# A graph layer's kernel: the experts' first rows prepared three chunks before the end of the node products

## The chip, the cores and the metric

The kernel runs on one core of one Trainium2 chip. The metric is the device time of one execution in microseconds. Three timed runs of the kernel before took 3494.83, 3513.76 and 3521.78 us; their median is 3513.76. One further execution was recorded by the hardware profiler, and its trace is what the text reads.

## What is computed

One layer of a graph network over 10000 rows of 512 numbers and 160000 weighted edges, in float32. Three parts follow each other: a graph product over the edges (a gather, a weighted sum by destination node, a product with W), a linear attention, and a mixture of experts whose weights are chosen once for the whole input.

```python
xn = _layernorm(x, axis=-1)
x = x + _L0_gnn_ref(xn, L0_gnn_W, L0_gnn_bias, edge_weight, src, dst) \
      + _L0_mix_ref((xn)[None], L0_mix_w_qkv, L0_mix_w_out, L0_mix_gamma)[0]
x = x + _L0_ffn_ref((_layernorm(x, axis=-1))[None], L0_ffn_router_w, L0_ffn_W1, L0_ffn_b1, L0_ffn_W2, L0_ffn_b2)[0]
```

Inside the graph product:

```python
h = jnp.matmul(X, W)
msgs = h[edge_src] * edge_weight[:, None]
agg = jax.ops.segment_sum(msgs, edge_dst, num_segments=X.shape[0])
return jax.nn.relu(agg + bias)
```

Inside the experts (six experts with a hidden width of 341 each; the kernel computes the first 1408 hidden units, eleven blocks of 128, for every row, and the rest only if the chosen weights need them):

```python
h = jax.nn.gelu(jnp.einsum('bsd,edf->ebsf', x, W1) + b1[:, None, None, :], approximate=False)
out_e = jnp.einsum('ebsf,efd->ebsd', h, W2) + b2[:, None, None, :]
return jnp.einsum('be,ebsd->bsd', expert_weights, out_e)
```

## The kernel before

**Tiles and stages.** Rows are worked on in 20 chunks, numbered 0 to 19: nineteen of 512 rows (128 partitions by 4 rows) and a last one of 272 (68 partitions). `NCH` is 20, so `NCH - 3` is chunk 17. The stages are: keys and queries with the first sums over edges; then, chunk by chunk, the attention's output (`attention`, products `po`), the node rows gathered from the edge sums (`gathered`, tile `at`), their transposition (`transposed`, `pt` to `aT`) and the node products with W (`pg`), which give the new rows `ot`, stored to DRAM as `x1_d` (`x_d` in the profile); then the experts, again chunk by chunk.

**The edges beside the chunks.** Until chunk 17 GpSimd gathers messages of 128 edges at a time (`msg`, line 584), TensorE sums them by a selection matrix (`pm`, line 602), ScalarE copies and stores the sums (`part`, lines 605 and 606). In the loop over chunks, chunk 17 begins with `all_edges_in` (defined above line 1014): the remaining edges are summed, the edge pools are closed, and `experts_weights` opens the pool of the experts' weights and loads them (sixteen loads of W1, line 305, one of W2, line 306, on SP). Then the last two chunks' node rows are gathered, and the attention of chunk 19 is computed with the transposition of chunk 17's rows in its middle.

**What a chunk ends with.** After its four node products a chunk adds bias, applies the ReLU and adds `ot` (lines 1090 and 1091), is stored (line 1092), and its mean and variance are found on VectorE with a square root on ScalarE (`row_stats`, lines 166 to 180, the root at 174). They are kept in `stats2`. A weighted sum of the rows goes to `xsum` (line 1103). Chunk 17 ends with `sums_of_weights`, four VectorE sums over W1 (lines 226 to 229 through the helper `sums_of`).

**The experts' rows.** The experts read the stored rows back in another layout: `rows_in` (line 328, four loads of 256 KB for a full chunk) brings them in squares of 32 by 32; `stats_of_squares` (line 337, four small TensorE products with the tile `squares`, and a ScalarE copy at 339) brings the statistics into the same layout; `normalising` (line 351) is sixteen ScalarE activations for a full chunk; `rows_turned` (line 367) is one VectorE transposition in blocks; `turned_in` (through `sums_for`, lines 233 to 236) makes four sums `xs`. The products of the experts use sums and differences of quarters, so they need both the rows `xnT` and the sums `xs`. `hidden` computes px, py and pz (all at line 243, the helper `product`), of which the last addition to px waits until VectorE has read it (`u`, lines 1290 and 1291). The activation function follows at line 1277.

**What sets the order.** TensorE runs in the order in which the program is written (`manual_schedule`). The other engines' orders come from a scheduler that ranks instructions by their place in the program and by when it expects them to be ready; each engine then runs its own queue in that order. Buffers are taken from pools in a stack; a tile that lies where a closed pool lay waits for the last users of that memory. Only the rows of chunk 0 are treated here: in the kernel before, their pool `f_in`, the tile `squares`, the loads, the normalising and the turning stand at the end of chunk 18 (lines 1110 to 1123):

```python
if c == NCH - 2:
    io_f["in"] = ctx.enter_context(tc.tile_pool(name="f_in", bufs=1, reuse_waits="tile"))
    ...
    xn = rows_in(0)
    ...
    turn = turned_in(0, rows_turned(0, xn))
```

The other chunks' rows are prepared inside the experts' loop, one chunk ahead.

Of the kernel before, what the change touches and what calls it, by code (L numbers as in the profile page):

```python
# [9 lines left out]
F32 = mybir.dt.float32  # L10
# [7 lines left out]
P = 128  # L18
SQ = 32
SPARE = 10  # L20
SUB = 4
# [35 lines left out]
def gps_layer_kernel(  # L57
# [19 lines left out]
    nc = tc.nc  # L77
# [19 lines left out]
    NCH = len(chunks)  # L97
# [6 lines left out]
    small = ctx.enter_context(tc.tile_pool(name="small", bufs=4))  # L104
# [3 lines left out]
    ident = const.tile([P, P], F32, name="ident")  # L108
# [181 lines left out]
    io_f = {}  # L290
    held_w = {}

    def experts_weights():
        wp = ctx.enter_context(tc.tile_pool(name="f_w", bufs=1, reuse_waits="tile"))
        w1_sb = held_w["w1"] = wp.tile([P, KB, NBASE * P], F32, name="w1_sb")
        w2_sb = held_w["w2"] = wp.tile([P, NBASE, D], F32, name="w2_sb")
        held_w["w1_sum"] = wp.tile([P, 4, KH, PAIRS * P], F32, name="w1_sum")
        b1_sb = held_w["b1"] = wp.tile([P, NF], F32, name="b1_sb")
        rw_sb = held_w["router"] = wp.tile([P, KB, NP], F32, name="rw_sb")
        nc.scalar.dma_start(rw_sb, router_t.rearrange("(k p) d -> p k d", p=P))  # L300
        nc.scalar.dma_start(b1_sb[:, : NF - 1], b1_a)
        nc.scalar.dma_start(b1_sb[: fsz[-1], NF - 1 :], b1_b)
        for j in range(KB):
            for g in range(P // SQ):
                nc.sync.dma_start(w1_sb[g * SQ : (g + 1) * SQ, j, :], features(w1)[j, g, :, : NBASE * P])
        nc.sync.dma_start(w2_sb, w2[: NBASE * P, :].rearrange("(f p) d -> p f d", p=P))
# [8 lines left out]
    def rows_in(c):  # L315

        r = chunks[c][1]
        xn = io_f["in"].tile([P, SUB, D], F32, name="xn2")
        if r % SQ:
            for j in range(KB):  # L320
                for g in range(P // SQ):
                    nc.sync.dma_start(xn[:r, :, j * P + g * SQ : j * P + (g + 1) * SQ],
                                      x1_d[c][:, :, g * P + j * SQ : g * P + (j + 1) * SQ])
        else:
            squares = x1_d[c].rearrange("(b t) s (g e) -> g t s b e", t=SQ, g=P // SQ)
            by = xn[:, :, : r // SQ * P].rearrange("p s (b e) -> p s b e", e=P)
            for g in range(P // SQ):
                nc.sync.dma_start(by[g * SQ : (g + 1) * SQ], squares[g])
        return xn

    def stats_of_squares(st, c0):


        n = st.shape[2]
        pst = psum.tile([P, P // SQ, n, SUB, 2], F32, name="pst", tag="ps")
        for b in range(P // SQ):
            nc.tensor.matmul(pst[:, b], io_f["squares"][:, b], stats2[:, c0 : c0 + n], start=True, stop=True,
                             skip_group_check=True)
        nc.scalar.copy(st, pst)

    def normalising(c, xn, st):

        r = chunks[c][1]

        def normal(s):
            if r % SQ:
                nc.scalar.activation(xn[:r, s, :], xn[:r, s, :], AF.Identity,
                                     bias=stats2[:r, c, s, 0:1], scale=stats2[:r, c, s, 1:2])
                return
            for b in range(r // SQ):  # L350
                nc.scalar.activation(xn[:, s, b * P : (b + 1) * P], xn[:, s, b * P : (b + 1) * P], AF.Identity,  # L351
                                     bias=st[:, b, s, 0:1], scale=st[:, b, s, 1:2])

        return [partial(normal, s) for s in range(SUB)]

    def rows_turned(c, xn):
        r = chunks[c][1]
        xnT = io_f["in"].tile([P, KB, SUB * P], F32, name="xnT")
        if r % SQ:
            for j in range(KB):  # L360
                pt = psum.tile([P, SUB * P], F32, name="pt", tag="ps")
                for s in range(SUB):
                    nc.tensor.transpose(pt[:, s * r : (s + 1) * r], xn[:r, s, j * P : (j + 1) * P],
                                        ident[:r, :r])
                (nc.scalar.copy if j % 2 else nc.vector.tensor_copy)(xnT[:, j, : SUB * r], pt[:, : SUB * r])
        else:
            nc.vector.transpose(
                xnT[:, :, : SUB * r].rearrange("p j (m t) -> p m j t", t=SQ),
                xn[:, :, : r // SQ * P].rearrange("p s (b j e) -> p (s b) j e", j=KB, e=SQ))
        return xnT  # L370

    def turned_in(c, xnT):
        h = 2 * chunks[c][1]
        xs = io_f["in"].tile([P, 4, KH, HALF], F32, name="xs")
        sums_for([xs[:, i, :, :h] for i in range(4)], xnT[:, :KH, :h], xnT[:, :KH, h : 2 * h],
                 xnT[:, KH:, :h], xnT[:, KH:, h : 2 * h])
        return xnT, xs
# [10 lines left out]
    with ExitStack() as ph:  # L388
# [222 lines left out]
        held = {"edges": []}  # L611
# [243 lines left out]
        xn = rows_of(0)  # L855
# [150 lines left out]
        def all_edges_in():  # L1006
            edges_to(NQ)
            carry(CARRIES[-1], NW - 1)
            assert not carried
            pools.clear()  # L1010
            edge_ctx.close()
            experts_weights()

        def gathered(c):
# [49 lines left out]
        for c, (_, r) in enumerate(chunks):  # L1064
            ot, at = mixed.pop(0), ats.pop(0)
            aT = io.tile([P, KB, SUB * P], F32, name="aT", bufs=1)

            if c == NCH - 3:
                all_edges_in()
                ats += [gathered(c + 1), gathered(c + 2)]  # L1070

            def nodes_rows():
                transposed(aT, at, r, psum, "ps", by_act=range(KB))

            if c + MIXED < NCH - 1:
                mixed.append(attention(c + MIXED, nodes_rows))
            elif c == NCH - 3:
                mixed.append(attention(NCH - 1, nodes_rows))
            else:
                nodes_rows()  # L1080
            if c < NCH - 3:
                ats.append(gathered(c + 1))
            if c == NCH - 4:
                held["last"] = queries_in(NCH - 1), rows_again(NCH - 1)

            for s in range(SUB):
                po = psum.tile([P, D], F32, name="pg", tag="ps")
                times(po, aT, s, r, wg)
                put_out(KB * PRODUCT)
                nc.vector.tensor_tensor(po[:r, :], po[:r, :], bias_b[:r], ALU.add)  # L1090
                nc.vector.scalar_tensor_tensor(ot[:r, s, :], po[:r, :], 0.0, ot[:r, s, :], op0=ALU.max, op1=ALU.add)
            nc.sync.dma_start(x1_d[c], ot[:r])
            mv = stats2[:, c]
            row_stats(ot, r, mv)

            if c == NCH - 1:
                normalize(wg, ot, r, mv)

            nc.vector.scalar_tensor_tensor(mv[:r, :, 0], mv[:r, :, 0], -1.0, mv[:r, :, 1],
                                           op0=ALU.mult, op1=ALU.mult)  # L1100
            if c < NCH - 1:
                for s in range(SUB):
                    nc.vector.scalar_tensor_tensor(xsum[:r], ot[:r, s, :], mv[:r, s, 1:2], xsum[:r],
                                                   op0=ALU.mult, op1=ALU.add)
                moved = small.tile([P, 1], F32, name="moved")
                nc.vector.tensor_reduce(moved[:r], mv[:r, :, 0], axis=AX.X, op=ALU.add)
                nc.vector.tensor_tensor(msum[:r], msum[:r], moved[:r], ALU.add)
            if c == NCH - 3:
                sums_of_weights()
            if c == NCH - 2:  # L1110
                io_f["in"] = ctx.enter_context(tc.tile_pool(name="f_in", bufs=1, reuse_waits="tile"))

                io_f["squares"] = io_f["in"].tile([P, P // SQ, P], F32, name="squares")
                for b in range(P // SQ):
                    nc.vector.tensor_copy(
                        io_f["squares"][:, b].rearrange("k (g t) -> k g t", t=SQ),
                        ident[:, None, b * SQ : (b + 1) * SQ].to_broadcast([P, P // SQ, SQ]))
                xn = rows_in(0)
                st = small.tile([P, P // SQ, 1, SUB, 2], F32, name="st_sq", bufs=1)
                stats_of_squares(st, 0)  # L1120
                for step in normalising(0, xn, st[:, :, 0]):
                    step()
                turn = turned_in(0, rows_turned(0, xn))
        in_order.close()
        query_ctx.close()

# [347 lines left out]
```

## Time and profile before

| What | us |
|---|---|
| timed runs: lowest, median, highest | 3494.83, 3513.76, 3521.78 |
| the profiled execution | 3295.9 |
| its span from first to last instruction | 3294.2 |
| TensorE busy in it | 3187.5 |
| VectorE busy | 1772.1 |
| ScalarE busy | 834.1 |
| GpSimd busy | 1317.8 |

The profiled execution is shorter than the timed ones; its mean granted TensorE clock is 0.985. All times of the trace are counted from the start of its span. A matmul of float32 appears in the trace as two records. In a row of the timeline the columns are the start, the length, the engine, the source line, the operation with output and inputs, the shapes, the number of instructions merged, and in brackets the idle time before it with what ended it. `x_d` stands for all of `x1_d`, `w_sb` for W1's, W2's and the edges' weights, `xn` for the experts' rows too. The stage of the edges ends at about 1845 us, that of the node products at about 1905 us; the experts take the rest.

### The profile page before, as it was taken

How to read it: one execution, taken by the hardware profiler on the slowest of the kernel's cores; microseconds unless marked ns; L12 is line 12 of the kernel's file. 1: busy time of each engine (PE TensorE's matmuls, PEld its weight loads, DVE VectorE, ACT ScalarE, POOL GpSimd, SP SyncE). 2: the span in 40 equal slices, each digit the busy share in tenths (PEclk: the TensorE clock that was granted, in tenths of full speed). 3: DMA queues.
4: the chain of work that ended last, by engine and by line, in shares of the span. 5: the costliest groups of instructions: out<-in, count | busy, mean ns of one | idle time of the engine just before them, and what ended most of it. 6: DMA issues, size and time to landing. Idle time of an engine off the chain costs nothing. (4 is left out here: it accounts for less than half of the span.)

```text
span 3294.2 us, 35223 instructions
## 1 busy us (share of the span) xinstructions
PE 3187.5 (97%) x12819; PEld 1898.0 (58%) x12819; DVE 1772.1 (54%) x3902; ACT 834.1 (25%) x1674; POOL 1317.8 (40%) x1421
## 2 busy tenths in 40 slices
PE   5899999999999999999999979999999999999998
PEld 3344444444443333333333358888888888888886
DVE  6655555555555366666665665455544554445532
ACT  5422222222222122222222132222222222222211
POOL 3377777777776777777777200000000000000000
PEclk8899999999999999999999989999999999999999
DMA  9678889888888999999999822121212212121111
GB/s 391 245 238 282 265 274 311 265 281 255 283 267 240 344 353 355 337 350 351 354 338 313 230 67 62 52 90 52 64 52 76 66 52 64 52 90 51 54 38 41
DMA packets 216728, 654.33 MB, mean 199 GB/s; under 512 B 34425, under 2 KB 74361, under 8 KB 188831
## 3 DMA queue, kind: packets, MB, share of 16 engines
q0 software_dynamic: 104096, 354.29, 32.9%
q1 hardware_dynamic: 69992, 175.33, 16.2%
q10 hardware_dynamic: 42452, 122.31, 9.6%
q8 instruction: 105, 1.72, 0.2%
q14 instruction: 83, 0.68, 0.1%
HBM read 491.21 MB, written 166.63 MB: 200 GB/s over the span
## 5 line engine op out<-in xcount | busy, mean ns | idle before, releaser
L584 POOL DMA_INDIRECT msg<-xn_d,src_sb x1250 | 1237.6, 990 | 422.9 <-issue 318.4
L602 PE MATMUL pm<-msg,sel 128*32 128x512 f32 x2504 | 357.7, 604 | 15.4 <-DMA msg<-xn_d,src_sb 14.4
L209 PE MATMUL pg<-wq,aT 128*128 128x512 f32 (+1 forms) x640 | 292.2, 604 | 0.0
L209 PE MATMUL po<-G,qT 128*128 128x512 f32 (+1 forms) x640 | 290.3, 600 | 1.4 <-DMA qT<-qT_d 1.4
L912 PE MATMUL pc<-xn,ek 128*128 128x512 f32 (+1 forms) x640 | 285.5, 596 | 0.0
L605 ACT COPY part<-pm 128x512 f32<-128x512 f32 x217 | 127.0, 585 | 618.3 <-PE pm L602 577.4
L602 PEld LDWEIGHTS pm<-msg,sel 128*32 128x32 f32 x2504 | 67.0, 109 | 273.0 <-issue 190.5
L209 PEld LDWEIGHTS pg<-wq,aT 128*128 128x128 f32 (+1 forms) x640 | 115.5, 188 | 176.1 <-issue 161.2
L243 PE MATMUL px<-xnT,w_sb 128*128 128x256 f32 (+1 forms) x800 | 204.9, 379 | 7.0 <-DVE u L1291 6.6
L209 PEld LDWEIGHTS po<-G,qT 128*128 128x128 f32 (+1 forms) x640 | 114.8, 187 | 164.7 <-issue 157.8
L166 DVE BATCH_NORM_STATS2 st<-ot 128x6 f32<-128x512 f32 (+1 forms) x160 | 110.4, 690 | 180.1 <-ACT ot L1053 179.3
L243 PE MATMUL p<-kq_sum,xs_b 128*128 128x512 f32 (+1 forms) x432 | 200.7, 600 | 0.0
L912 PEld LDWEIGHTS pc<-xn,ek 128*128 128x128 f32 (+1 forms) x640 | 118.0, 191 | 139.3 <-issue 131.4
L243 PE MATMUL px<-w_sb,hh 128*128 128x256 f32 (+1 forms) x800 | 185.8, 379 | 0.0
L243 PE MATMUL py<-xs,w_sum 128*128 128x256 f32 (+1 forms) x800 | 185.7, 375 | 0.0
L243 PE MATMUL py<-w_sum,hh 128*128 128x256 f32 (+1 forms) x800 | 179.2, 379 | 0.0
L243 PEld LDWEIGHTS px<-xnT,w_sb 128*128 128x128 f32 x800 | 150.8, 192 | 30.1 <-DVE u L1291 10.2
L243 PEld LDWEIGHTS px<-w_sb,hh 128*128 128x128 f32 (+1 forms) x800 | 150.2, 188 | 22.8
L243 PEld LDWEIGHTS py<-w_sum,hh 128*128 128x128 f32 (+1 forms) x800 | 150.0, 188 | 22.7
L243 PEld LDWEIGHTS py<-xs,w_sum 128*128 128x128 f32 x800 | 150.2, 191 | 20.1
L243 PEld LDWEIGHTS p<-kq_sum,xs_b 128*128 128x128 f32 (+1 forms) x432 | 78.0, 187 | 116.1 <-issue 89.6
L351 ACT ACTIVATE xn<-xn,st_all 128x128 f32<-128x128 f32 x288 | 114.8, 481 | 97.3 <-DMA xn<-x_d 97.3
(298 smaller groups left out, 4566.8 us busy)
## 6 DMA issues: line engine op xcount, KB each, us to landing
part_d<-part ACTq DMA_DIRECT2D x217, 256.0 KB
msg<-xn_d,src_sb POOLq DMA_INDIRECT x1250
xn<-in_x SPq DMA_DIRECT2D x19, 1024.0 KB
xn_d<-xn ACTq DMA_DIRECT2D x19, 1024.0 KB
qT_d<-qT ACTq DMA_DIRECT2D x19, 1024.0 KB
qT<-qT_d SPq DMA_DIRECT2D x19, 1024.0 KB
xt<-in_x SPq DMA_DIRECT2D x19, 1024.0 KB
x_d<-ot SPq DMA_DIRECT2D x19, 1024.0 KB
```

Source lines behind the costliest of these rows:

```text
L166: nc.vector.bn_stats(st[:r, s, :], t[:r, s, :])
L209: nc.tensor.matmul(po[:r, :], t[:, kb, s * r : (s + 1) * r], w[:, kb, :], start=kb == 0, stop=kb == KB - 1)
L243: nc.tensor.matmul(o, lhs[j], rhs[j], start=start and j == 0, stop=stop and j == n - 1, skip_group_check=True)
L351: nc.scalar.activation(xn[:, s, b * P : (b + 1) * P], xn[:, s, b * P : (b + 1) * P], AF.Identity, bias=st[:, b, s, 0:1], scale=st[:, b, s, ...
L584: nc.gpsimd.indirect_dma_start(out=m[k], out_offset=None, in_=xn_d, in_offset=bass.IndirectOffsetOnAxis(ap=src_sb[:, t0 + k : t0 + k + 1], ...
L602: nc.tensor.matmul(pm[h * WIN : (h + 1) * WIN, :], sel[:, k, :], m[k] if k < len(m) else m[0], start=j == 0, stop=j == batch - 1, skip_gro ...
L605: nc.scalar.copy(part, pm)
L912: nc.tensor.matmul(pc, ek[:r, s, cb * P : (cb + 1) * P], xn[:r, s, :], start=s == 0, stop=s == SUB - 1)
```

## The change

The pool `f_in` is opened and the four loads of chunk 0's rows are put in between the closing of the edge pools and the loading of the experts' weights. The rest (the tile `squares`, the statistics in squares, the normalising, the transposition and the sums) moves from the end of chunk 18 to the middle of chunk 17, just ahead of its node products and behind the attention of chunk 19. No operation is added or left out.

```diff
@@ -1009,6 +1009,8 @@
             assert not carried
             pools.clear()
             edge_ctx.close()
+            io_f["in"] = ctx.enter_context(tc.tile_pool(name="f_in", bufs=1, reuse_waits="tile"))
+            held["first_rows"] = rows_in(0)
             experts_weights()
 
         def gathered(c):
@@ -1083,6 +1085,18 @@
             if c == NCH - 4:
                 held["last"] = queries_in(NCH - 1), rows_again(NCH - 1)
 
+            if c == NCH - 3:
+                io_f["squares"] = io_f["in"].tile([P, P // SQ, P], F32, name="squares")
+                for b in range(P // SQ):
+                    nc.vector.tensor_copy(
+                        io_f["squares"][:, b].rearrange("k (g t) -> k g t", t=SQ),
+                        ident[:, None, b * SQ : (b + 1) * SQ].to_broadcast([P, P // SQ, SQ]))
+                xn = held.pop("first_rows")
+                st = small.tile([P, P // SQ, 1, SUB, 2], F32, name="st_sq", bufs=1)
+                stats_of_squares(st, 0)
+                for step in normalising(0, xn, st[:, :, 0]):
+                    step()
+                turn = turned_in(0, rows_turned(0, xn))
             for s in range(SUB):
                 po = psum.tile([P, D], F32, name="pg", tag="ps")
                 times(po, aT, s, r, wg)
@@ -1107,20 +1121,6 @@
                 nc.vector.tensor_tensor(msum[:r], msum[:r], moved[:r], ALU.add)
             if c == NCH - 3:
                 sums_of_weights()
-            if c == NCH - 2:
-                io_f["in"] = ctx.enter_context(tc.tile_pool(name="f_in", bufs=1, reuse_waits="tile"))
-
-                io_f["squares"] = io_f["in"].tile([P, P // SQ, P], F32, name="squares")
-                for b in range(P // SQ):
-                    nc.vector.tensor_copy(
-                        io_f["squares"][:, b].rearrange("k (g t) -> k g t", t=SQ),
-                        ident[:, None, b * SQ : (b + 1) * SQ].to_broadcast([P, P // SQ, SQ]))
-                xn = rows_in(0)
-                st = small.tile([P, P // SQ, 1, SUB, 2], F32, name="st_sq", bufs=1)
-                stats_of_squares(st, 0)
-                for step in normalising(0, xn, st[:, :, 0]):
-                    step()
-                turn = turned_in(0, rows_turned(0, xn))
```

In the text, line numbers are those of the kernel before.

## The prediction

> **What bounds the kernel now.** I read the page's first part, then TensorE's waits from 1780 us to the end, then the timelines of the engines round the longest wait, then the windows.
>
> ```profile
> PE 3187.5 (97%) x12819; PEld 1898.0 (58%) x12819; DVE 1772.1 (54%) x3902; ACT 834.1 (25%) x1674; POOL 1317.8 (40%) x1421
> ```
>
> TensorE is busy for 97% of the span, so an edit outside its work gains only what TensorE idles. From 1780 us on it waited for:
>
> ```profile
> PE px L243 <- DVE xs L235: 13.5, 1, 13.5
> PE pm L602 <- DMA msg<-xn_d,src_sb: 11.7, 8, 2.6
> PE px L243 <- DVE u L1291: 6.6, 5, 3.6
> ```
>
> The columns are total us, times, longest. One wait of 13.5 us, for the sums `xs` of the experts' first rows, is the longest. TensorE's timeline shows where it lies:
>
> ```profile
> 1876.03 13.90 PE L209 MATMUL pg<-wq,aT 128*128 128x512 f32 x32
> 1889.76 0.95 PE L337 MATMUL pst<-stats,squares 128*128 128x8 f32 x8
> ...
> 1891.60 13.90 PE L209 MATMUL pg<-wq,aT 128*68 128x512 f32 x32
> 1919.02 2.05 PE L243 MATMUL px<-xs,w_sum 128*128 128x256 f32 x4 [13.52 <-DVE xs L235]
> ...
> 1926.29 1.03 PE L243 MATMUL px<-xnT,w_sb 128*128 128x256 f32 x4
> ```
>
> The last node product ends at about 1905.5, the first expert product starts at 1919.02. Who held up `xs`? ScalarE, then VectorE:
>
> ```profile
> 1908.13 0.20 ACT L174 ACTIVATE root<-ve 68x4 f32<-68x4 f32 x1 [11.15 <-DVE ve L169]
> 1908.27 6.26 ACT L351 ACTIVATE xn<-xn,st_sq 128x128 f32<-128x128 f32 x16
> ```
>
> ```profile
> 1911.10 0.16 DVE L1099 SCALAR_TENSOR_TENSOR stats<-stats 68x4 f32<-68x4 f32 x1
> 1914.57 2.31 DVE L367 STREAM_TRANSPOSE xnT<-xn 128x2048 f32<-128x2048 f32 x1 [3.31 <-ACT xn L351]
> 1916.98 0.69 DVE L233 TENSOR_TENSOR xs<-xnT 128x512 f32<-128x512 f32 x1
> ```
>
> The normalising stands in ScalarE's queue behind the root of the *last* chunk's statistics, and these end after the last product. So 6.26 us of normalising, 2.4 of transpose and 2.6 of sums follow one another with TensorE idle. The loads did not decide it: two of the four were issued by 1834.4, the other two at 1894.36 to 1896.4, behind the store of chunk 18.
>
> **What the Trainium skill says.** "TensorE: Matmul & The Clock Gate", section "Architectural detail: the array is 16× 32×32, not 1× 128×128", says that ScalarE's and VectorE's queues are strictly first in, first out. The trace agrees: the activations start 0.14 us after the root. The same page, section "Part 1: The HAM clock gate", says that an idle TensorE falls to half clock and needs a busy window to return. The windows agree (length, PE, PEld, DVE, ACT, POOL busy, then granted clock, DMA share, GB/s):
>
> ```profile
> 1890.00:1906.00 16.00, 15.50 (x55) 5.95 (x54) 14.81 (x32) 1.65 (x6) 3.19 (x42) 1.00 0.40 100
> 1906.00:1919.00 13.00, 0.00 (x0) 0.01 (x1) 8.96 (x19) 6.41 (x17) 0.00 (x0) 0.63 0.58 203
> 1919.00:1930.00 11.00, 10.98 (x49) 9.60 (x50) 4.38 (x9) 4.15 (x8) 0.00 (x0) 0.81 0.68 96
> ```
>
> "DMA: Bandwidth & Descriptors", section "Issuing engines are not separate DMA queues", says that all queues share sixteen engines; in the edges' tail (1834.4 to 1844) their share reads 1.02 at 324 GB/s, so a load there delays the gathers.
>
> **The change, part by part**, from the order in which each engine's instructions stand in the changed program, and the rows above.
>
> *SP.* Four row loads of 256 KB, together, now stand ahead of the sixteen W1 loads and the W2 load, and wait for the last gather, since their tile lies in memory of the edge pools. SP's own waits put the end of the gathers at 1844.0. The four leave there at a median 0.63 us each, the later ones also after stores of edge sums (the longest such wait of a row load was 3.6 us). At 261 GB/s (window 1860 to 1871) 1 MB takes 4.0 us: landed by about 1853. W1 moves back by the same 4.0 us: its sum L227 started at 1871.2 after a DMA wait of 0.58, so W1 is there by 1875; L227 now comes about 1882.8 in VectorE's queue. Cost 0, cover 7.6 us. Gone from the tail is 0.5 MB of row loads: at 324 GB/s at most 1.6 us less waiting for gathers, at least 0. I take half, **0.8 us**.
>
> *POOL.* Nothing is moved. The combining of edges and two gathers of node rows now share the engines with row loads instead of W1; their data is needed at 1875, unchanged. I take 0.
>
> *TensorE.* Four statistics products (8 records) go ahead of chunk 17's node products: they took 0.81 us from their start to the next, and take it there. Sum 0; three chunks of node products are 0.81 us later and end at 1905.5 as before.
>
> *ScalarE.* The copy (0.19) and 16 activations (6.26) now follow the root of the last attention, at 1862.7: they end at 1869.0. The next item is the copying of `aT` for chunk 18, which started at 1874.97 and now needs 1875.8. Cover 6.8 us, cost 0.
>
> *VectorE.* The four `squares` copies (0.63 together at 1832.3) now stand there and among the statistics of chunk 19's attention, behind an idle time of 16.39 us: 0. The transpose (2.41 from start to start) and four sums (2.6) now come at about 1870, among chunk 17's additions; I call it 5.0. Between 1866.5 and 1911.3 VectorE's waits that can take them are 0.58 + 0.54 + 0.56 + 0.46 = 2.1 us. So its end of the last chunk, 1911.26, becomes 1911.3 + 5.0 - 2.1 = 1914.2. While it lags, TensorE's products wait for buffers: chunk 18's first products need the third addition of chunk 17, done by my count at 1875.4 and needed at 1876.8. Close, but 0. Three of the four W1 sums (L226, L228, L229, 1887.87 to 1893.35 before) fall back behind chunk 19's first addition: by my count the last two end at 1903.9 and 1906.0. The first expert product needs the former at 1905.5, `pz` the latter at 1909: 0, with 1.6 us of cover; and since `u` stands behind them on VectorE, a delay here is the same delay as there, not a second one.
>
> *The new end.* TensorE starts the first expert products at 1905.5 instead of 1919.02. Up to the product that needs `u` there are 24 records of 0.216 us (1.73 per 8 in the chain) = 5.2 us: 1910.7. There it waits for the addition `u` (L1291), which stands behind the last chunk on VectorE: 1914.2 + 0.42, with 0.3 for handing over, = 1914.9. Before, this product ran at 1926.29. Gain 1926.3 - 1914.9 = **11.4 us**. What is late next is thus `u`, about 4.2 us of idle. Half clock no longer follows so long a gap; that is contained in the difference. Later waits (2.71 for the router's row, 1.16 for the W2 sums) hang on the same start and stay. The next chunk's loads follow the last store on SP; they landed in time when issued at 1916.9 to 1919.5, and now go at about 1911. Their activations stand a little later among the first units on ScalarE, which was busy 7.76 of 10 us there (1930 to 1940) and kept no product waiting: 0. The three small loads of the router's weights and biases on ScalarE's queue go at about 1849 as before.
>
> Sum: 11.4 + 0.8 = **12.2 us** of the profiled execution's 3295.9 (span 3294.2), thus 3283.7. The timed runs stand 6.6% above that execution (median 3513.76), and no page shows where. I subtract 12 from the median: **3502 us**, 0.34% faster.
>
> **The rivals.**
>
> *VectorE takes over.* If the 2.1 us of waits can't be used and `squares`, transpose and W1 sums bunch up, `u` comes some 5 us later. For it: VectorE is busy 14.81 of 16 us up to 1906. Gain 7: 3507.
>
> *The idle stretch costs the timed runs more.* They are 217.9 us longer than the profile. If that excess came from slow clock after idle stretches in proportion to TensorE's idle time (3294.2 - 3187.5 = 106.7 us), 13.5 / 106.7 of it, 27.6 us, would go too: 12 + 27.6 gives 3474, faster by 1.1%. For it: 0.63 and 0.81 above. Against: the clock is back at 1.00 by 1930.
>
> *Slower: rows late in front of `aT`.* The activations stand ahead of chunk 18's `aT` copies on ScalarE, and whatever they wait for holds TensorE. If the rows land later than 1869.5, each us costs one; from 1881.7 on the kernel is slower than before. Landing at 1900 would give 30.5 - 12.2 = 18 us, 3532. For it: the loads wait for stores and share engines that are full until 1877. Against: only 1 MB, 25 us to land in. That the loads do not move early at all, because their memory is freed late, is the same case with a harmless end, 3514.
>
> **How the numbers follow.** A measurement of this kernel can tell about 1% from no change (35 us; the three runs span 27). Forecast 0.52; VectorE 0.13; clock 0.24; late rows 0.11. The forecast with the runs' spread (-19, +8) reaches 3483 to 3510; the clock's case pulls the low end to 3472, part of the late case the high end to 3522. Faster by over 1%: 0.19 of the clock's case, 0.10 of the forecast, 0.01 of VectorE's = 0.30. Slower: 0.05 late rows, 0.03 from spread = 0.08. Within 1%: 0.62.
>
> **What would show it.** Right: no wait of `px` for `xs`; one of about 4 us for `u`; ScalarE's 16 activations ending near 1869, the transpose near 1870; the L227 sum without a DMA wait. Wrong: TensorE's `pt` or `pg` of chunks 17 and 18 waiting for ScalarE or VectorE, a longer wait for gathers, or a wait for `u` over 9 us.

## The result, and the profile after

The change makes the kernel 0.46% faster: median 3491.08 us (22 runs) against 3509.72 us (22 runs) before, ratio 0.9954, 95% interval 0.9937 to 0.9971, so a gain of 10 to 22 us (the two medians differ by 18.6). It is within 1%, and the predicted 3502 is 11 us too high; 4 of these are the base, which was 3513.76 in the three runs shown. The profiled execution took 3479.5 us (span 3477.7), but its edges end at 2044.75 instead of 1845.01. To compare stages I use one measure throughout, the **stretch**: from the start of the first `po` product of chunk 19's attention to the start of the expert product that needs `u`. All work that was moved lies in there, but for the `squares` copies and two of the row loads, which stood in the edges' tail.

TensorE's timeline of the kernel after, in the columns used before:

```profile
2044.75 10.52 PE L209 MATMUL po<-G,qT 128*68 128x512 f32 x24
...
2060.28 0.95 PE L337 MATMUL pst<-stats,squares 128*128 128x8 f32 x8
2061.09 13.98 PE L209 MATMUL pg<-wq,aT 128*128 128x512 f32 x32
...
2105.12 1.03 PE L243 MATMUL px<-xs,w_sum 128*128 128x256 f32 x4
...
2112.92 1.13 PE L243 MATMUL px<-xnT,w_sb 128*128 128x256 f32 x4 [2.45 <-DVE u L1291]
```

The last product of chunk 19 runs straight into `px`: no wait for `xs` is left. The only wait is for `u`, 2.45 us. The stretch is 2112.92 - 2044.75 = 68.17 us; before, it is 1926.29 - 1845.01 = 81.28. So 13.1 us went, where 11.4 were forecast: the wait of 13.5 and 1.9 that the first expert products lost at a lower clock behind it (granted 0.81 from 1919 to 1930; 7.27 us up to the product for `u`, now 5.35), less the new 2.45.

ScalarE and then VectorE after (L1104 and L1105 are the bias and the addition that stood at L1090 and L1091, L1113 is the old L1099):

```profile
2062.23 0.21 ACT L174 ACTIVATE root<-ve 68x4 f32<-68x4 f32 x1 [0.77 <-DVE ve L169]
2062.71 6.28 ACT L351 ACTIVATE xn<-xn,st_sq 128x128 f32<-128x128 f32 x16 [0.27 <-DMA w_sb<-in_w]
2075.55 2.05 ACT L203 COPY aT<-pt 128x512 f32<-128x512 f32 x4 [6.56 <-PE pt L201]
```

```profile
2066.21 0.69 DVE L1104 TENSOR_TENSOR pg<-pg,bias_b 128x512 f32<-128x512 f32 x1
2066.93 0.69 DVE L1105 SCALAR_TENSOR_TENSOR ot<-pg,ot 128x512 f32<-128x512 f32 x1
...
2069.59 2.30 DVE L367 STREAM_TRANSPOSE xnT<-xn 128x2048 f32<-128x2048 f32 x1
...
2075.38 0.70 DVE L1104 TENSOR_TENSOR pg<-pg,bias_b 128x512 f32<-128x512 f32 x1
2075.98 0.69 DVE L166 BATCH_NORM_STATS2 st<-ot 128x6 f32<-128x512 f32 x1
2076.58 0.68 DVE L1105 SCALAR_TENSOR_TENSOR ot<-pg,ot 128x512 f32<-128x512 f32 x1
...
2081.84 1.49 DVE L227 TENSOR_TENSOR w_sum<-w_sb 128x1280 f32<-128x1280 f32 x1
...
2112.45 0.41 DVE L1291 TENSOR_TENSOR u<-u,px 128x256 f32<-128x256 f32 x1
```

The activations follow the attention's root and end at 2068.99; ScalarE is then idle for 6.56 us before it must copy `aT`, so they cost nothing. W1's first sum starts without a wait for a transfer. VectorE has hardly any gaps (the longest wait between 2066 and `u` is 0.31 us): the rows at 2075.38, 2075.98 and 2076.58, each of which needs nothing of the one just ahead of it, are 0.60 apart, while the dependent pair at 2066.21 and 2066.93 is 0.72 apart. That is where the prediction mis-sized a term.

### The profile page after: what moved, and what is told of

Same layout as the page of the kernel before. It is cut to its first block, busy times and chain, and to the rows that moved or that the text cites. A ratio compares the mean times of both kernels' runs of the same rounds, so it can differ in the third digit from the quotient of the medians.

```text
span 3477.7 us, 35221 instructions
## 1 busy us (share of the span) xinstructions
PE 3259.1 (94%) x12819; PEld 1917.7 (55%) x12819; DVE 1764.0 (51%) x3902; ACT 831.0 (24%) x1674; POOL 1323.8 (38%) x1421
## 5 line engine op out<-in xcount | busy, mean ns | idle before, releaser
L209 PE MATMUL po<-G,qT 128*128 128x512 f32 (+1 forms) x640 | 305.9, 616 | 24.7 <-issue 23.2
L912 PE MATMUL pc<-xn,ek 128*128 128x512 f32 (+1 forms) x640 | 309.4, 634 | 10.5 <-issue 7.7
L912 PEld LDWEIGHTS pc<-xn,ek 128*128 128x128 f32 (+1 forms) x640 | 125.7, 204 | 170.0 <-issue 158.5
L166 DVE BATCH_NORM_STATS2 st<-ot 128x6 f32<-128x512 f32 (+1 forms) x160 | 110.1, 689 | 137.6 <-issue 74.3
L590 DVE TENSOR_TENSOR sel<-iota_w,place 128x128 f32<-128x128 f32 (+2 forms) x217 | 74.5, 344 | 194.5 <-remote 74.2
L243 PE MATMUL p<-wk,xnT 128*128 128x512 f32 (+1 forms) x288 | 142.7, 618 | 18.4 <-issue 16.3
```

The source lines that it names most:

```text
L166: nc.vector.bn_stats(st[:r, s, :], t[:r, s, :])
L209: nc.tensor.matmul(po[:r, :], t[:, kb, s * r : (s + 1) * r], w[:, kb, :], start=kb == 0, stop=kb == KB - 1)
L243: nc.tensor.matmul(o, lhs[j], rhs[j], start=start and j == 0, stop=stop and j == n - 1, skip_group_check=True)
L590: nc.vector.tensor_tensor(sel[:, :n], iota_w[:, None, :].to_broadcast([P, n, WIN]), place[:, t0 : t0 + n, None].to_broadcast([P, n, WIN]), ...
L912: nc.tensor.matmul(pc, ek[:r, s, cb * P : (cb + 1) * P], xn[:r, s, :], start=s == 0, stop=s == SUB - 1)
```

## The experiments

Each was timed beside the kernel before on one chip, and on these chips that kernel takes 3296 to 3299 us (5 to 22 runs of each, 11 to 52 of before); the row of the change's first profile repeats the comparison above. Line numbers in a run's rows are those of its own kernel. "Wait" is TensorE's wait just ahead of the product that ends the stretch, "behind" the time from that product to the first `pmean` product; both come from one profile of each kernel. The timed gain is (1 - ratio) times the median of before that was measured with it.

| Run | stretch | wait for `u` | behind | ratio, 95% interval | timed gain |
|---|---|---|---|---|---|
| before, first profile | 81.28 | none | 8.79 | | |
| b1, before again | 81.64 | none | 8.79 | 0.9997 (0.9988 to 1.0005) | 1.0 |
| the change, first profile | 68.17 | 2.45 | 8.89 | 0.9954 (0.9937 to 0.9971) | 16 |
| a1, the change again | 68.17 | 2.44 | 12.20 | 0.9958 (0.9944 to 0.9971) | 13.9 |
| e1, only loads early | 74.49 | 1.03 | 8.89 | 0.9974 (0.9963 to 0.9984) | 8.6 |
| e2, loads late | 74.52 | none | 8.79 | 0.9977 (0.9970 to 0.9985) | 7.6 |
| e7, normalising last | 83.95 | none | 8.78 | 0.9999 (0.9990 to 1.0007) | 0.3 |
| e8, turning last | 79.44 | none | 8.78 | 0.9988 (0.9982 to 0.9995) | 4.0 |
| f2, rows behind weights | 94.81 | 0.96 | 8.90 | 1.0025 (1.0018 to 1.0033) | -8.2 |
| e4, W1's sums on GpSimd | 75.80 | 0.96 | 8.89 | 0.9981 (0.9971 to 0.9990) | 6.3 |
| e5, last rows on GpSimd | 74.61 | 8.88 | 12.93 | 0.9981 (0.9974 to 0.9989) | 6.3 |
| e6, both | 79.97 | 7.49 | 10.54 | 0.9995 (0.9986 to 1.0003) | 1.6 |
| f3, as e5, product moved | 74.61 | 8.89 | 12.80 | 0.9977 (0.9970 to 0.9985) | 7.6 |
| f5, as f3, tied | 65.95 | 0.23 | 9.85 | 0.9935 (0.9918 to 0.9952) | 21.4 |

**Which part pays: e1, e2, e7, e8.** My theory was that the order on ScalarE and VectorE decides. The rival was that the loads' time does.

e1 moves the loads alone and leaves the rest at the end of chunk 18 (against the kernel before; `...` stands for lines left out):

```diff
             edge_ctx.close()
+            io_f["in"] = ctx.enter_context(tc.tile_pool(name="f_in", bufs=1, reuse_waits="tile"))
+            held["first_rows"] = rows_in(0)
             experts_weights()
...
             if c == NCH - 2:
-                io_f["in"] = ctx.enter_context(tc.tile_pool(name="f_in", bufs=1, reuse_waits="tile"))
...
-                xn = rows_in(0)
+                xn = held.pop("first_rows")
```

> Only the pool and the four row loads are moved ahead of the weights; the statistics products, the normalising and the turning stay written at the end of chunk 18. Measure: the stretch from the first attention product of chunk 19 after the edges to the first px product that waits for u (81.3 us before, 68.2 after). Theory: what pays is the place of the activations and of the transposition in their queues, not the loads as such. With the rows there early the activations now stand ahead of the copies of chunk 19's aT on ScalarE, behind statistics products that TensorE makes only after chunk 18's, so TensorE waits some 8 to 10 us for ScalarE before chunk 19's node products; the wait for xs is gone. Stretch 75 to 78 us, about half of the gain, ratio 0.998. Rival (the loads alone bring the gain): 68 us, no wait for aT, ratio 0.995. Rival (loads alone bring nothing): 81 us, the wait for xs of 13 us stays.

TensorE's timeline of e1:

```profile
1898.53 15.38 PE L209 MATMUL pg<-wq,aT 128*68 128x512 f32 x32 [6.14 <-ACT aT L203]
```

Half of the gain came with the loads alone. With the rows there early, the program's scheduler itself set the activations ahead of chunk 19's `aT` copies on ScalarE, where they made TensorE wait 6.14 us; no wait for `xs` was left.

e2 is the opposite: the rest as in the change, the loads written with it and thus behind the weights in the program (this diff and those below are against the changed kernel).

```diff
             edge_ctx.close()
-            io_f["in"] = ctx.enter_context(tc.tile_pool(name="f_in", bufs=1, reuse_waits="tile"))
-            held["first_rows"] = rows_in(0)
...
             if c == NCH - 3:
+                io_f["in"] = ctx.enter_context(tc.tile_pool(name="f_in", bufs=1, reuse_waits="tile"))
...
-                xn = held.pop("first_rows")
+                xn = rows_in(0)
```

> The statistics products, normalising and turning stand ahead of chunk 17's node products as in the change, but the pool and the loads are written with them, behind the weights' loads. Theory: two of the four loads then go behind the W2 load, the activations move behind the root of chunk 18 and the transposition among the last chunk's statistics; TensorE waits for xs some 8 us instead of 13.5 and not for u. Stretch (81.3 before, 68.2 after) 73 to 74 us, ratio 0.997 to 0.998. Rival (only the place in the program counts, not the loads): 68 us, ratio 0.995. Rival (late rows hold ScalarE and with it aT): over 81 us, a wait of TensorE for aT.

ScalarE's and TensorE's timelines of e2:

```profile
1901.94 6.25 ACT L351 ACTIVATE xn<-xn,st_sq 128x128 f32<-128x128 f32 x16
```

```profile
1917.37 2.05 PE L243 MATMUL px<-xs,w_sum 128*128 128x256 f32 x4 [7.00 <-DVE near L178]
```

The stretch is e1's, 74.5 us. The activations now stood behind chunk 18's root, which started at 1901.82, and waited for no load there; so VectorE had the transposition late, at 1912.91, and `px` waited 7.00 us. Each part alone brings half; only together do they give the activations the place that is covered.

e7 and e8 keep all loads and statistics early and hold one step back by an order tied by hand: in e7 the activations (and what follows them) go behind the last chunk's root on ScalarE, in e8 only transposition and sums go behind its statistics on VectorE.

```diff
                 stats_of_squares(st, 0)
-                for step in normalising(0, xn, st[:, :, 0]):
-                    step()
-                turn = turned_in(0, rows_turned(0, xn))
...
+            if c == NCH - 1:
+                held["behind"] = held["root"]
+                for step in normalising(0, xn, st[:, :, 0]):
+                    step()
+                held.pop("behind")
+                turn = turned_in(0, rows_turned(0, xn))
```

(In e8 the first two removed lines stay, and `held["behind"]` is the last chunk's L1113.)

> Everything as in the change, loads and statistics products early, but the sixteen activations are tied behind the root of the last chunk's statistics on ScalarE, where they stood before. Theory: the gain is gone though the rows are there 50 us early; TensorE waits for xs 12 to 14 us; stretch 80 to 82 us (81.3 before, 68.2 after), ratio 0.999 to 1.001. Rival (early loads or the relief of the edges' end bring part of it): stretch under 79 us or a ratio under 0.998.

> Everything as in the change, with the activations early, but the transposition and its four sums are tied behind the last chunk's statistics on VectorE. This parts ScalarE's share of the gain from VectorE's. Theory: ScalarE's 3.3 us of the old wait are gone, VectorE's 5 us come after the last chunk again, so TensorE waits about 10 us for xs and then runs at a low clock for a while: stretch 76 to 79 us (81.3 before, 68.2 after), ratio 0.998 to 0.999. Rival (the activations were the whole delay): 70 us or less, ratio 0.996.

TensorE's timeline of e7, then of e8:

```profile
1922.21 2.05 PE L243 MATMUL px<-xs,w_sum 128*128 128x256 f32 x4 [15.25 <-DVE xs L235]
```

```profile
1920.04 2.05 PE L243 MATMUL px<-xs,w_sum 128*128 128x256 f32 x4 [11.54 <-DVE xs L235]
```

With the rows loaded early, and with nothing undone but the place of the activations and what must follow them, the wait for `xs` is back at 15.25 us (before: 13.52), and the gain is gone: 0.3 us timed, interval across zero. Releasing the activations but not the transposition returns only 4.5 of the 15.8 us between e7 and the change (83.95 - 79.44, 83.95 - 68.17). Both stretches are a little longer than I expected (80 to 82, 76 to 79). So early data is worth nothing without the place in both queues.

**The rival on the slower side: f2.** The loads go behind W1 and W2 on SP, and the activations keep their place ahead of `aT`.

```diff
-            held["first_rows"] = rows_in(0)
             experts_weights()
+            held["first_rows"] = rows_in(0)
...
+            if held.get("tie"):
+                behind(one, held["act"])
```

> The changed kernel with its four row loads behind those of W1 and W2 on SP instead of ahead of them, and the copies of aT for chunk 18 tied behind the activations, so that the activations keep their place. Theory (the loads' place decides as soon as the activations stand ahead of aT): the rows land behind W1, some 31 to 35 us after the first node product of the last attention, instead of before 18; the activations end 6.3 us later, TensorE waits 6 to 12 us for aT of chunk 18, VectorE catches up meanwhile and the wait for u goes to under 1. Stretch 73 to 79 instead of 68.2, so that most of the 13.1 us is lost. Rival (rows arrive in time anyway, as 1 MB among 7 on shared engines): no wait for aT, stretch 68 to 70.

ScalarE's and then TensorE's timeline of f2:

```profile
1898.79 6.26 ACT L353 ACTIVATE xn<-xn,st_sq 128x128 f32<-128x128 f32 x16 [17.03 <-DMA xn<-x_d]
```

```profile
1905.57 16.97 PE L211 MATMUL pg<-wq,aT 128*128 128x512 f32 x32 [24.91 <-ACT aT L203]
```

The rows came later than I expected, 1898.79 - 1848.59 = 50.2 us into the stretch rather than 31 to 35, since SP took until 1891.9 to issue the four; this run does not show what held it. TensorE then stood for 24.9 us, and the kernel is slower than before by 0.25%, interval 0.18 to 0.33. In the change's profile the activations start 18.0 us into the stretch and have 6.56 us of cover; the rows came 50.2 - 18.0 - 6.6 = 25.6 us later than that, and the stretch grew by 26.6: 24.9 of wait, 3.1 because the products behind it took 16.97 us instead of 13.90, less 1.5 of the wait for `u`. The mechanism of that rival is thus real. It needs late rows and the place ahead of `aT` together: f2 holds that place by the tie, while in e2, with late loads and no tie, the scheduler put the activations elsewhere and `aT` was not held up.

**The change where the kernel takes 3297 us, and before again: a1, b1.** Neither program is edited.

> The changed kernel unaltered, timed on the chip of the other runs of this call. Theory (the change gains what TensorE no longer waits, 13.1 us by the first profile, and 1 to 3 us more before): ratio about 0.995 to 0.996 whatever the kernel's time on that chip is. The stretch from the first node product of the last attention after the edges to the product that waits for u: 68 us, with a wait for u of about 2.5 us. Rival (part of the 16 us belongs to the long executions of the first chip, where the kernel took about 3510): where the kernel takes about 3296, the gain is 11 us or less.

> The kernel before, unaltered, for its profile on the chip of these runs. Theory: stretch 81.3 as in the first profile, xs waited for by 13.5 us, and about 1365 us from the product that waits for u to the end as in all others (the 1367.9 of the first profile is spread of one execution). Rival: 1368 again; then before loses 3 us more behind the product, and this explains why timed gains are some 3 us larger than the stretch's. Ratio 1.000.

The stretches repeat, 68.17 and 81.64. The gain of 13.9 us at 3297 us is that of the first comparison within both intervals. Its own interval, 9.6 to 18.5, still reaches the rival's 11, but the two pairs of profiles differ by 13.1 and 13.5 us in the stretch, so nothing shows that the gain belongs to the long executions. From the product that ends the stretch to the end, b1 took 3296.4 - 1928.12 = 1368.3 us, which is the rival's number; but before took 1367.9, the change 1364.8 and a1 1369.1: one kernel differs by 4 us from itself, and no part of the gain can be read there. In a1 most of this is clock, told below.

**Can the last wait go too: e4, e5, e6, f3, f5.** `u` waits for VectorE, so work was taken off VectorE: in e4 W1's four sums (1.4 us each), in e5 the last chunk's normalising (L184, 1.91 us), in e6 both.

```diff
-                w1_sb[:, :KH, q_half], w1_sb[:, KH:, q_half])
+                w1_sb[:, :KH, q_half], w1_sb[:, KH:, q_half], engine=nc.gpsimd)
...
-                normalize(wg, ot, r, mv)
+                normalize(wg, ot, r, mv, pool=SUB)
```

> The changed kernel with the four sums of W1 on GpSimd. Theory (VectorE's backlog sets u): VectorE loses 4 x 1.4 = 5.6 us of work ahead of u, so u is limited by the last chunk's own statistics and normalising; the wait for u falls from 2.5 to about 1, the stretch from 68.2 to about 67; ratio to before 1 us lower than that of the change. Rival (GpSimd is late, or slows VectorE): the W1 sums end after the first expert product is ready, px waits for w_sum on GpSimd, stretch 70 or more.

> The changed kernel with the last chunk's normalising (four instructions, L184) on GpSimd. Theory: 1.9 us leave VectorE's queue ahead of u, u comes about 1.9 us earlier, wait for u about 0.6, stretch about 66.3. Rival: GpSimd's four take several us and the sum of the normalised rows (pmean) waits for them; then the wait moves to the product behind and the kernel is no faster than the change.

> Both: W1's sums and the last chunk's normalising on GpSimd. Theory: VectorE is ahead, TensorE does not wait for u at all; stretch 60.4 + 5.2 = 65.7, that is 2.5 us less than the change; ratio to before about 0.0008 lower than the change's. Rival: GpSimd's queue, with both, becomes the bound: px waits for w_sum or the product of the means for the normalised rows, by more than 2.5 us.

All three were misses: each has a longer stretch than the change. In e4 GpSimd's sums bar VectorE. GpSimd's and VectorE's timelines of e4:

```profile
1864.83 2.88 POOL L227 TENSOR_TENSOR w_sum<-w_sb 128x1280 f32<-128x1280 f32 x1 [0.40 <-DMA w_sb<-in_w]
...
1878.48 3.23 POOL L228 TENSOR_TENSOR w_sum<-w_sum,w_sb 128x1280 f32<-128x1280 f32 x1
```

```profile
1865.31 2.43 DVE L169 TENSOR_SCALAR ve<-mv 68x4 f32<-68x4 f32 x1
...
1878.88 3.38 DVE L234 TENSOR_TENSOR xs<-xnT 128x512 f32<-128x512 f32 x1
```

A `ve` that takes 0.17 us elsewhere lasts until GpSimd's sum ends; two of the `xs` sums take 3.4 instead of 0.68. Chunk 18's products then wait 6.19 us for an addition. "SBUF — State Buffer" of the Trainium skill, section "SBUF: two separate sides", says that VectorE and GpSimd share a pair of ports as an exclusive lock, and that the loser "fully blocks"; these rows agree.

In e5 VectorE waits instead. Its timeline:

```profile
1917.09 0.16 DVE L1113 SCALAR_TENSOR_TENSOR stats<-stats 68x4 f32<-68x4 f32 x1 [8.51 <-POOL wq L184]
1917.17 0.41 DVE L1291 TENSOR_TENSOR u<-u,px 128x256 f32<-128x256 f32 x1
```

L1113 overwrites the means that GpSimd's four are still reading (8.28 us against 1.91 on VectorE), and `u` stands behind it. e6 has both: TensorE waits 3.5 us in three places for additions, and 7.49 us for `u`. f3 therefore moves that product of the last chunk to `mean_row`, the router's step that makes the mean, beside e5's own edit:

```diff
-            nc.vector.scalar_tensor_tensor(mv[:r, :, 0], mv[:r, :, 0], -1.0, mv[:r, :, 1],
-                                           op0=ALU.mult, op1=ALU.mult)
             if c < NCH - 1:
+                nc.vector.scalar_tensor_tensor(mv[:r, :, 0], mv[:r, :, 0], -1.0, mv[:r, :, 1],
+                                               op0=ALU.mult, op1=ALU.mult)
...
+        mv = stats2[:, NCH - 1]
+        nc.vector.scalar_tensor_tensor(mv[:r, :, 0], mv[:r, :, 0], -1.0, mv[:r, :, 1],
+                                       op0=ALU.mult, op1=ALU.mult)
         mean_ctx.close()
```

> The last chunk's normalising on GpSimd as in e5, but the in-place product on VectorE that waited for it (L1113 of the last chunk) goes behind it, to the means of the rows; u has nothing of GpSimd ahead of it. Theory (e5 lost by that wait alone): u comes 1.9 to 2.1 us earlier than in the change, wait for u under 1, stretch 66 to 67. Rival (GpSimd's operation bars VectorE's while it runs, as W1's sums in e4 did to VectorE's xs): u or the sums behind it wait up to 2.1 us for each of GpSimd's four, and the stretch is 68 to 70 or the wait appears just behind u.

A miss that says nothing of either theory: nothing held the product back, the scheduler put it ahead of `u` again, and it waited 8.51 us as in e5. f5 ties it.

```diff
+        behind(one, held["first_hh"])
```

> As f3, with the in-place product on VectorE (L1174 here) really tied behind the first pair's last sum of hh; in f3 it had gone back ahead of u. Theory (e5 and f3 lost by VectorE waiting for GpSimd's four, and by nothing else): u follows the last chunk's statistics directly, at 65.5 to 66 us of the stretch, the wait for u is under 0.6, and stretch 66 to 66.6, 1.6 to 2.1 us less than the change's 68.2; ratio to before 0.0005 lower than the change's, which these rounds can hardly tell from it. GpSimd's four end at about 74, before the means need them at 84. Rival (GpSimd's four bar VectorE, as W1's sums did in e4): u, or v and hh behind it, wait for one of GpSimd's four, up to 2.1 us each, and the stretch is 68 or more, or the next pair's product waits that much.

VectorE's, GpSimd's and TensorE's timelines of f5:

```profile
1906.03 0.41 DVE L1295 TENSOR_TENSOR u<-u,px 128x256 f32<-128x256 f32 x1
...
1909.06 0.42 DVE L226 TENSOR_TENSOR hh<-h,hh 128x256 f32<-128x256 f32 x1 [0.57 <-ACT h L1281]
...
1914.75 0.16 DVE L1174 SCALAR_TENSOR_TENSOR stats<-stats 68x4 f32<-68x4 f32 x1 [4.04 <-POOL wq L184]
```

```profile
1906.31 8.40 POOL L184 TENSOR_SCALAR wq<-ot,stats 68x512 f32<-68x512 f32 x4 [48.06 <-PE pz L243]
```

```profile
1906.50 1.13 PE L243 MATMUL px<-xnT,w_sb 128*128 128x256 f32 x4 [0.23 <-DVE u L1295]
...
1915.29 1.13 PE L243 MATMUL px<-xnT,w_sb 128*128 128x256 f32 x4 [0.70 <-DVE u L1295]
```

`u` follows the statistics, the wait is 0.23 us, and the stretch is 65.95, 2.2 us below the change's. About 1 us of that comes back at once: the tied product still waits 4.04 us for GpSimd, the second pair's `u` stands behind it, and TensorE waits 0.70 us for that ("behind" is 9.85 us instead of 8.89). f5 is 16 to 27 us faster than before, by its interval. That it also beats the change is shown by the stretch with what lies behind it, 1.3 us, in one profile of each; by time alone the intervals overlap (0.9918 to 0.9952 and 0.9944 to 0.9971), and the difference of the two gains, 7.5 us, is more than the stretch explains.

## Why the prediction was right, step by step

- **What bounds it.** Right: the 13.5 us wait for `xs` was the cost, and the place behind the last root its cause (e7 brings it back by itself). "The loads did not decide it" was right for the arrival of the data and wrong for the order: where the loads stand decides which place the scheduler gives the activations (e1, e2).
- **SP.** The rows were in time, the activations waiting 0.27 us at most, though SP took 8.9 us to issue the four (2040.24 to 2049.12) where 2.5 were counted. L227 was forecast at 37.8 us of the stretch without a wait; it came at 2081.84 - 2044.75 = 37.1. One reading behind this was wrong: the 0.58 us ahead of L227 before are put down to the gather of node rows, not to W1's load (`[0.58 <-DMA at<-part_d,row_of]` in VectorE's row at 1871.20). e4, whose GpSimd takes up W1's sums as the loads land, shows the cover: L227 could start 1864.83 - 1848.02 = 16.8 us and L226, after waiting 7.79 us for W1, 27.5 us into the stretch.
- **TensorE.** The statistics products took 0.81 us there as here. `px` was forecast 60.5 us into the stretch and started at 60.4, and reached the product for `u` at 65.7, as computed.
- **ScalarE.** Forecast: the activations end 24.0 us into the stretch, with 6.8 of cover. Measured 24.2 and 6.56.
- **VectorE.** The term that was mis-sized. Of the 5.0 us put in, I let only the 2.1 us of its visible waits absorb any, so that the last chunk would end 2.9 us later. It ended 67.8 us into the stretch against 66.3 before, 1.5 us later. From chunk 17's first addition on, the two timelines give the sum: the transposition and the four sums took 4.6 us from start to start, and the waits shrank by 1.6 (2.7 to 1.1). What I had put at nothing is the spacing: the 36 additions and statistics (L1090, L1091, L166) took 22.3 us instead of 24.1, because more of them now stand next to instructions they do not depend on, 0.60 us apart, where before dependent ones followed at 0.73. 4.6 - 1.6 - 1.8 leaves 1.2; small operations make up the rest. Hence 2.45 us of wait for `u` instead of 4.2, and 13.1 us instead of 11.4.
- **The gathers' tail, 0.8 us.** Open. Apart from the change's first profile, the first `po` product starts anywhere from 1839.85 to 1849.84, so one profile of each says nothing at this size; most timed gains lie about 1 to 6 us above the stretch's, which the runs don't explain. So it is the stretch that bears the prediction out: that the total came within 11 us says little, where single runs of one kernel differ by 36 us and more.
- **Half clock "no longer follows so long a gap".** Right in the first profile, wrong as a rule: see below.
- **The rivals.** VectorE did not take over: the wait was under the forecast. The late rows did not occur, but f2 shows their price. The clock's case, that 27.6 us more would go in the long executions, falls: the gain is 16 us in them and 13.9 without them. The kernel after happened to be profiled in such an execution. Windows of before (1000 to 1845) and after (1000 to 2000), in the columns of the prediction's windows:

```profile
1000.00:1845.00 845.00, 823.14 (x2910) 309.68 (x2908) 486.62 (x1235) 183.91 (x345) 626.43 (x629) 0.99 0.94 334
```

```profile
1000.00:2000.00 1000.00, 924.78 (x3232) 352.71 (x3230) 524.68 (x1296) 200.59 (x372) 682.49 (x682) 0.95 0.86 296
```

TensorE is idle for 75 of 1000 us there against 22 of 845, and the transfers run at 296 GB/s instead of 334: the excess lies ahead of the stretch, where the change alters nothing but two loads and the `squares` copies. From `px` to the end both profiles agree to 3 us (3294.2 - 1919.02 = 1375.2, 3477.7 - 2105.12 = 1372.6).

## What to carry to other kernels

A step with its data at hand still runs only where it stands in its engine's queue: look for the row with a long wait that is followed at once by unrelated work of the next stage, and move that work to a place where the same engine idles and the next item has slack. Price what you insert into a nearly full engine by how its neighbours' spacing changes too, not by its visible waits alone, and look at what the product behind will wait for next. When work is put on another engine, look for an instruction that overwrites its input and stands ahead of the critical one: in e5 and f3 a product of 0.16 us held VectorE, and `u` behind it, for 8.5 us.

## What the hardware showed unexpectedly

**Half clock after a short wait.** The change and a1 are one program with the same wait (2.45 and 2.44 us). TensorE's timeline of the change, then of a1:

```profile
2113.88 1.90 PE L337 MATMUL pst<-stats,squares 128*128 128x80 f32 x16
```

```profile
1916.59 1.40 PE L243 MATMUL px<-xnT,w_sb 128*128 128x256 f32 x4 [2.44 <-DVE u L1291]
1917.78 3.53 PE L337 MATMUL pst<-stats,squares 128*128 128x80 f32 x16
```

In a1 the products behind it ran at half speed for some 5 us, 3.3 us lost (12.20 - 8.89); in the change's profile nothing was lost. A second place shows the same. In all 14 profiles TensorE waits 2.7 us for the router's row `e_row`, and the eight records of `ph` behind it take 3.70 us in five of them and 5.17 to 6.71 in nine (in the five the lower clock comes later: ten records of `px` behind the next wait take 3.5 to 4.0 us, where seven of the nine take 2.43). Before and b1 are one program too, and both wait 2.71 us. TensorE's timeline of before, then of b1:

```profile
1962.65 5.40 PE L243 MATMUL ph<-xnT,w_sb 128*128 128x512 f32 x8
```

```profile
1964.48 3.70 PE L243 MATMUL ph<-xnT,w_sb 128*128 128x512 f32 x8
```

"TensorE: Matmul & The Clock Gate" of the Trainium skill, section "Part 1: The HAM clock gate", says that the window that sets the clock runs freely, so that where it falls differs between runs, which would fit. It puts half clock after an idle window of about 3.4 us; here the measurement differs, since a wait of 2.44 us was enough.

**GpSimd beside VectorE depends on the operation.** While W1's sums (two inputs) ran in e4, `ve` and two of the `xs` sums stood until they ended, though the transposition beside L226 (at 1875.13) took its usual 2.30 us. The normalising in f5 (one input and two scalars) held up nothing: `hh`, like `xs` with two inputs in SBUF, took 0.42 us in the middle of it, the same as in the change. So the lock that e4's rows agree with does not show in f5; these two runs do not tell what decides it.

**Whole-core stalls.** In the change's profile TensorE, VectorE and ScalarE stand still together for up to some 10 us in the edges while gathers go on: the last time up to 2040 us, when their idle times were 9.5, 10.8 and 10.0 us. ScalarE's waits up to 2040 us:

```profile
ACT part L605 <- remote: 254.5, 43, 11.5
```

Before and a1 have no such row among their largest, and the same kernel before took 3510 us in one comparison and 3296 to 3299 in the others. No run here tells the cause.
